# Sums of the scores' stationary quarters moved to DRAM, in a four-layer graph network on one core

## The chip, the cores and the metric

The kernel runs on one core of a Trainium2 chip. The metric is the device time of one execution in microseconds (us). The kernel before has a median of 2388.08 us in three runs (2387.78 to 2389.01). A core has five engines: TensorE (PE; its weight loads are shown apart, as PEld), VectorE (DVE), ScalarE (ACT), GpSimd (POOL) and SyncE (SP), and 16 DMA engines. SP does nothing here but issue DMAs.

## The reference

The input is a matrix `x` of 2708 nodes with 512 features and a symmetric 0/1 matrix `adj` with few ones. Four layers follow each other, and each is `x = layernorm(x + layer(x))`:

```
deg = max((adj != 0).sum(-1), 1)
layer 0: relu((dinv * (adj + I) * dinv @ x + x) @ W + b)       # the degree enters by dinv = rsqrt(deg)
layer 1: (dis[:, None] * adj * dis[None, :] @ x) @ W.T + b
layer 2: twice:  Wh, Ws = split(x @ W)
                 a = softmax(Wh @ Ws.T) * adj
                 x = leaky_relu(a @ Wh + x)
layer 3: adj @ (x @ W) + b, eight heads side by side
```

The change touches layer 2, the two attention layers, and a few instructions after layer 3.

## The kernel before, in words

**Tiles and chunks.** The 2708 nodes are 22 blocks of 128 rows (the last has 20). Columns are cut into six chunks (`CH`): four of 512, one of 384, one of 276. Nearly all SBUF is one pool, `pages`: 87 buffers of 2 KB in each of the 128 partitions. Every large tile takes a page by `self.page(...)` and gives it back after its last access. A second pool of 11 wider buffers (`wides`) holds what is gathered. PSUM is used as two sets of four banks.

**Order.** The class `Ordered` wraps all engines: each engine keeps its instructions in just the order in which the Python code issues them. As one helper issues everything, nearly all lines of the profile are L71; instructions are told apart by the names of their tiles. Numbers of buffers are left out of the names, so the tile `s1_0_3` of a sum and the score tile `s0_1_3` are both `s`.

**An attention layer.** `project_steps` makes, for each chunk, `wst` (four pages a chunk: the stationary side of the scores, `z @ mixed`) and the rows `z`, which go to DRAM (`pairs`). For the scores, the product of `wst` with a moving chunk `xs` is done, for chunks 0 to 4, with seven half products instead of eight (`product`, `PRODUCTS`). For that, `wst` is seen as quarters a11, a12, a21, a22, and `sum_weights` makes three sums, s1 = a21 + a22, s2 = s1 - a11, s4 = a12 - s2. A fourth, s3 = a11 - a21, overwrites a21 (`replace`), whose old content is kept in DRAM (`quarter`) and fetched back by `restore` before chunk 5, which is done with plain products (`scores`). Each of the four wide groups of blocks (k = 0 to 3) has one page each for s1, s2 and s4, so 12 pages hold sums from the projection to the end of chunk 4. Groups 4 and 5 have theirs in one page each.

**The loop of the scores.** `layer` runs over the six chunks, and `pair_steps` over the pairs of blocks, two pairs to a wide group, ten pairs a chunk. A pair is seven products on TensorE (tiles `spx`, `spy`), with ScalarE's copies to the score pages `s` and `v` between. Product 1 comes first, then the older pair's 7, then 2 and 5 (5 reads s1), then the older pair's 4, then 6 (s2) and 3 (s4). Beside it, the chunk before is softened: VectorE subtracts the maximum, ScalarE takes the exponential, VectorE sums it and multiplies by the mask `a`, and SP writes the result to `pairs` in DRAM (`pairs<-s`). When the whole chunk is written, POOL gathers rows of `pairs` by indirect DMAs (`g<-pairs,givers`, some 42 a chunk), and TensorE multiplies them (`acc<-g`, `weigh`). At most ten gathers are ahead of their products. `load_moving` fetches the next chunk's `xs`, `load_mask` the masks.

**The end.** The flags that `examine` leaves in `bad` tell whether the input is of the form that this program supports. After layer 3 `other_weights` sums them: `tensor_reduce` over a row, a product with a float32 matrix of ones `every` (L467, L471) over the partitions, `flag` (L473). All engines load the flag (L474) and branch over the general program (L2196), and a closing barrier follows (L2234). `every` lies in a pool of its own, which is opened after the others are closed.

Of the kernel before, what the change touches and what calls it, by code (L numbers as in the profile page):

```python
# [8 lines left out]
FP = mybir.dt.float32  # L9
FR = mybir.dt.float32r  # L10
BF = mybir.dt.bfloat16
# [8 lines left out]
P = 128  # L20
# [33 lines left out]
class Ordered:  # L54


    def __init__(self, tc):
        self.tc, self.last = tc, {}
        for name in ("tensor", "vector", "scalar", "gpsimd", "sync"):
            setattr(self, name, OrderedEngine(self, getattr(tc.nc, name)))  # L60
# [27 lines left out]
class Kernel:  # L88
# [369 lines left out]
    def other_weights(self):  # L458


        nc = self.nc
        with (
            self.tc.tile_pool(name="ps_bad", bufs=1, space=PSUM) as ps_bad,
            self.tc.tile_pool(name="all", bufs=1) as pool,
        ):
            every = pool.tile([P, P], FP, tag="every", name="every")
            nc.vector.memset(every, 1.0)  # L467
            total = self.small.tile([P, 1], FP, tag="bad_sum", name="bad_sum")
            nc.vector.tensor_reduce(total, self.bad, AX.X, ALU.add)
            ps = ps_bad.tile([P, 1], FP, tag="bad", name="bad_ps")  # L470
            nc.tensor.matmul(ps, every, total, start=True, stop=True)  # L471
            flag = self.small.tile([P, 1], I32, tag="flag", name="flag")
            nc.vector.tensor_scalar_min(flag, ps, 1.0)  # L473
        return nc.values_load(flag[0:1, 0:1])  # L474
# [8 lines left out]
def pairs_of(k):  # L483


    return {4: (1, P), 5: (1, P)}.get(k, (2, 2 * P))


SOFT = NB + 2
ALONE = 18  # L490
SEVEN = [k for k in range(len(CH)) if CH[k][1] >= 384]
# [909 lines left out]
class AttentionLayer:  # L1401
    def __init__(self, number, pairs):
        self.number, self.pairs = number, pairs
        self.w, self.mixed, self.xt, self.wst = [], [], {}, {}
        self.sums, self.second, self.plain = {}, {}, set()


class Attention:
# [7 lines left out]
    def __init__(self, fast):  # L1416
        self.f, self.k, self.nc = fast, fast.k, fast.nc
        self.page, self.bank = fast.page, fast.bank
        tc = self.k.tc
        self.scratch = self.k.ctx.enter_context(  # L1420
            tc.tile_pool(name="pairs", bufs=1, space=DRAM)
        )

        self.pairs = [
            [
                self.scratch.tile([NP, 2 * PAIR + D], FP, tag=f"p{a}{b}", name=f"pairs{a}{b}")
                for b in range(2)
            ]  # L1430
            for a in range(2)
        ]
        self.mixed = self.scratch.tile([DC, P, D], FP, tag="mixed", name="mixed")
        self.quarter = [
            [
                self.scratch.tile(
                    [2, P, pairs_of(k)[0] * P], FP, tag=f"q{a}_{k}", name=f"quarter{a}_{k}"
                )
                for k in range(len(CH))
            ]  # L1440
            for a in range(2)
        ]
        self.layers = [AttentionLayer(a, self.pairs[a]) for a in range(2)]
        self.clock, self.fetch_free, self.pending = 0.0, 0.0, []
# [143 lines left out]
    def sum_weights(self, ly, k):  # L1588

        nc, a = self.nc, ly.number
        wide = pairs_of(k)[0] * P
        a11, a21, a12, a22 = self.quarters(ly, k)
        names = ("s1", "s2", "s4")
        if k < 4:
            tiles = {n: self.page(f"{n}_{a}_{k}", FP, (P, 2, wide)) for n in names}
            tiles = {n: [t[:, c, :] for c in range(2)] for n, t in tiles.items()}
        else:
            t = self.page(f"s12_{a}_{k}", FP, (P, 4, P))  # L1600
            free = CH[k][1]
            tiles = {
                "s1": [t[:, c, :] for c in range(2)],
                "s2": [t[:, 2 + c, :] for c in range(2)],
                "s4": [ly.wst[k][c][:, free : free + P] for c in range(2)],
            }
        for c in range(2):
            nc.vector.tensor_add(tiles["s1"][c], a21[c], a22[c])
            nc.vector.tensor_sub(tiles["s2"][c], tiles["s1"][c], a11[c])
            nc.vector.tensor_sub(tiles["s4"][c], a12[c], tiles["s2"][c])  # L1610
            nc.sync.dma_start(self.quarter[ly.number][k][c], a21[c])
        ly.sums[k] = {"a11": a11, "a12": a12, "a22": a22, "s3": a21, **tiles}
        ly.plain.add(k)

    def replace(self, ly, k):
        if k in ly.plain:
            ly.plain.remove(k)
            t = ly.sums[k]
            for c in range(2):
                self.nc.vector.tensor_sub(t["s3"][c], t["a11"][c], t["s3"][c])  # L1620
# [51 lines left out]
    def pair_steps(self, ch):  # L1672


        nc, h, cw = self.nc, ch.half, ch.cw
        pairs = [(k, b) for k in range(len(CH)) for b in range(pairs_of(k)[0])]
        blocks = lambda p: [CH[p[0]][0] // P + p[1] + i * pairs_of(p[0])[0] for i in range(2)]
        old = None

        def begin(p):  # L1680
            name = f"{ch.name}_{p[0]}_{p[1]}"
            t = {
                "x": self.bank(0, f"spx{name}")[:, :h],
                "y": None,
                "v": self.page(f"v{name}"),
                "j": blocks(p),
                "p": p,
                "name": name,
            }
            for i, j in zip(("s", "r"), t["j"]):  # L1690
                t[i] = ch.s[j] = self.page(f"s{ch.name}_{j}")
            return t

        def seven(t):
            self.product(ch, t["p"], 7, t["x"])
            nc.scalar.copy(t["v"][:, :h], t["x"])

        def four(t):
            self.product(ch, t["p"], 4, t["x"])
            nc.scalar.copy(t["r"][:, :h], t["x"])  # L1700

        def first_block(t):
            nc.vector.tensor_add(t["s"][:, :cw], t["s"][:, :cw], t["y"][:, :cw])
            ch.complete.append(t["j"][0])

        def second_block(t):
            nc.vector.tensor_add(t["r"][:, h:cw], t["r"][:, h:cw], t["v"][:, :h])
            ch.complete.append(t["j"][1])

        for p in pairs:  # L1710
            self.replace(ch.ly, p[0])
            t = begin(p)
            self.product(ch, p, 1, t["x"], start=True)
            nc.scalar.copy(t["s"][:, :h], t["x"])
            yield "mid"
            if old:
                seven(old)
            t["y"] = self.bank(0, f"spy{t['name']}")
            self.product(ch, p, 2, t["y"][:, :h], start=True)
            self.product(ch, p, 5, t["y"][:, h:cw], start=True)  # L1720
            nc.scalar.copy(t["r"][:, h:cw], t["y"][:, h:cw])
            if old:
                first_block(old)
            yield "end"
            if old:
                four(old)
            yield "mid"
            self.product(ch, p, 6, t["x"])
            nc.scalar.copy(t["s"][:, h:cw], t["x"])
            self.product(ch, p, 3, t["y"][:, h:cw])  # L1730
            if old:
                second_block(old)
            old = t
            yield "end"
        seven(old)
        yield "mid"
        first_block(old)
        four(old)
        second_block(old)
        yield "end"  # L1740
# [190 lines left out]
    def fetch_ahead(self):  # L1931
        count = sum(len(c.fetched) for c in self.chunks)
        for c in self.chunks:
            while c.to_fetch:
                if c.softened < SOFT or count >= self.AHEAD:
                    return
# [129 lines left out]
    def layer(self, ly, chunks, fill):  # L2066
        f = self.f
        self.chunks, self.made = chunks, {}
        for k, ch in enumerate(chunks):
# [4 lines left out]
            for what in self.walk(ch):  # L2074
                if what == "mid":
                    if old and n >= 2 and old.softened < SOFT:
                        self.soften(old)
# [8 lines left out]
                if old and n >= 3:  # L2086
                    for _ in range(n % 3 == 0 if ch.seven else 1 + n % 2):
                        if old.softened < SOFT:
                            self.soften(old)
# [21 lines left out]
                if old and n == 2:  # L2111
                    self.shift_columns(old)
            assert not old or old.softened == SOFT
        last = chunks[-1]
# [13 lines left out]
        done = self.clock + (2 if ly.number == 0 else 4)  # L2128
        while last.softened < SOFT:
            self.soften(last)  # L2130
# [107 lines left out]
```

## Time and profile before

| | |
|---|---|
| median of three runs | 2388.08 us |
| the profiled execution: its own time | 2392.95 us |
| its span, first to last instruction | 2391.1 us |
| mean granted TensorE clock | 0.976 |
| TensorE busy | 2250.5 us, 94% of the span |
| VectorE, ScalarE, POOL busy | 1544.5, 723.8, 709.0 us |
| moved by DMA | 491.80 MB, mean 206 GB/s |

The numbers are of one execution. The profile shows for each engine when it was busy and what ended its idle time before an instruction ("a <- b" in the view of the waits: a waited, b released it). The chain of waits goes back from the last instruction, at each step to what released it. Along the span, layers 0 and 1 take until about 595 us, the projection of the first attention layer until 760, its scores until 1280, the second's projection until 1490, its scores and weighing until about 2070, and layer 3 the rest.

### The profile page before, as it was taken

What the parts mean: (1) busy time and instruction counts of PE and PEld (TensorE: products, weight loads), DVE (VectorE), ACT (ScalarE), POOL (GpSimd) and SP (SyncE); (2) the same over time, 40 slices, a digit from 0 to 9 for tenths busy, and PEclk for the clock granted to TensorE, in tenths of its full rate; (3) what the DMA queues carried; (4) which work ended last, traced back from release to release, by engine and by line L of the source; (5) the groups of instructions that cost most, each with busy time, mean ns of one, the idle gap of its engine ahead of it and who ended that gap; (6) DMA issues with size and microseconds to landing.
All of it is one profiled execution on the core that took longest, in us unless ns stands there. A gap on an engine that the chain in (4) does not pass through costs nothing.

```text
span 2391.1 us, 29254 instructions
## 1 busy us (share of the span) xinstructions
PE 2250.5 (94%) x9725; PEld 1523.5 (64%) x9725; DVE 1544.5 (65%) x3180; ACT 723.8 (30%) x1654; POOL 709.0 (30%) x827
## 2 busy tenths in 40 slices
PE   9999999999999998898989999998989896899996
PEld 6767866778445876566764445876565763376684
DVE  6777787776746598666964512588788975355423
ACT  7443442222111242232322101243233322151211
POOL 2433511111000003544456440002635464543000
PEclk9999999999999999999999999999999998999998
DMA  9976732225476036767789998225968889784310
GB/s 342 278 202 183 219 104 78 77 75 190 161 260 254 10 100 204 266 232 241 267 300 333 340 401 315 71 75 173 296 207 267 273 286 317 238 258 139 108 55 32
DMA packets 267858, 491.80 MB, mean 206 GB/s; under 512 B 41006, under 2 KB 132838, under 8 KB 267696
## 3 DMA queue, kind: packets, MB, share of 16 engines
q1 hardware_dynamic: 199040, 274.87, 33.3%
q0 software_dynamic: 68656, 214.96, 28.1%
q8 instruction: 78, 1.28, 0.2%
q14 instruction: 84, 0.69, 0.1%
HBM read 310.17 MB, written 179.54 MB: 205 GB/s over the span
## 4 chain that ended last, share of the span: by engine, by line
PE 74%; DVE 12%; issue 5%; DMA 4%; another core or an unknown queue 2%; ACT 2%; POOL 1%; SPq 0%; DVEq 0%; POOLq 0%; ACTq 0%
PE acc L71 30%; PE spx L71 11%; PE mm L71 8%; PE spy L71 7%; PE wst L71 6%; PE z L71 6%; DVE s L71 4%; PE sp L71 3%; DVE sum L71 2%; DVE top L71 1%; DMA at<-in_adj_t 1%; DMA x<-in_x 1%; POOL g L71 1%; DMA pairs<-s 1%
## 5 line engine op out<-in xcount | busy, mean ns | idle before, releaser
L71 POOL DMA_INDIRECT g<-pairs,givers x510 | 527.3, 1034 | 962.0 <-PE acc L71 283.7
L71 PE MATMUL acc<-m,xh 128*128 128x512 f32 (+4 forms) x1584 | 566.0, 379 | 2.5 <-ACT m L71 1.6
L71 PE MATMUL acc<-m,xl 128*128 128x512 f32 (+4 forms) x1584 | 549.8, 365 | 6.3 <-DVE xl L71 6.3
L71 PEld LDWEIGHTS acc<-m,xh 128*128 128x128 f32 (+1 forms) x1584 | 288.3, 188 | 64.2 <-issue 19.2
L71 PEld LDWEIGHTS acc<-m,xl 128*128 128x128 f32 (+1 forms) x1584 | 288.6, 188 | 50.7 <-DVE xl L71 6.7
L71 PE MATMUL acc<-g 128*32 128x512 f32 (+1 forms) x1020 | 280.6, 621 | 11.2 <-DMA g<-pairs,givers 9.5
L71 PE MATMUL mm<-w,ht 128*128 128x512 f32 (+1 forms) x528 | 223.1, 593 | 0.0
L71 PE MATMUL spx<-xs,wst_sb 128*128 128x256 f32 (+1 forms) x800 | 192.7, 380 | 19.2 <-ACT s L71 15.7
L71 ACT CAST m<-at 128x512 fp32r<-128x512 uint8 (+5 forms) x396 | 198.8, 566 | 37.0 <-DMA at<-mask 27.3
L71 ACT COPY s<-spx 128x256 f32<-128x256 f32 (+1 forms) x300 | 107.0, 360 | 334.8 <-PE spx L71 219.9
L71 DVE TENSOR_TENSOR s<-s,a 128x512 f32<-128x512 f32 (+3 forms) x264 | 166.0, 629 | 48.5 <-DMA a<-mask 24.5
L71 ACT ACTIVATE s<-s 128x512 f32<-128x512 f32 (+3 forms) x264 | 152.2, 581 | 132.1 <-DVE s L71 119.0
L71 PEld LDWEIGHTS spx<-xs,wst_sb 128*128 128x128 f32 x800 | 148.8, 195 | 67.8 <-issue 23.3
L71 DVE TENSOR_TENSOR sum<-sum,s 128x512 f32<-128x512 f32 (+4 forms) x252 | 156.7, 622 | 49.2 <-ACT s L71 26.8
L71 PEld LDWEIGHTS acc<-g 128*32 128x32 f32 (+1 forms) x1020 | 79.2, 137 | 143.7 <-issue 103.5
L71 PEld LDWEIGHTS mm<-w,ht 128*128 128x128 f32 (+1 forms) x528 | 95.7, 186 | 116.5 <-issue 112.2
L71 DVE TENSOR_TENSOR s<-s,shift 128x512 f32<-128x512 f32 (+3 forms) x264 | 162.3, 619 | 9.2 <-ACT shift L71 4.9
L71 PE MATMUL z<-w,xt 128*128 128x512 f32 (+1 forms) x352 | 152.2, 598 | 0.0
L71 DVE TENSOR_TENSOR top<-top,s 128x512 f32<-128x512 f32 (+4 forms) x240 | 149.5, 623 | 2.3
L71 PE MATMUL wst<-xt,mixed 128*128 128x512 f32 (+2 forms) x384 | 150.9, 545 | 0.0
L71 PE MATMUL spx<-t,wst_sb 128*128 128x256 f32 (+1 forms) x400 | 107.8, 394 | 43.4 <-ACT v L71 27.2
L71 PE MATMUL sp<-xs,wst_sb 128*128 128x276 f32 (+5 forms) x512 | 131.3, 460 | 12.2 <-ACT s L71 12.1
(190 smaller groups left out, 2713.3 us busy)
## 6 DMA issues: line engine op xcount, KB each, us to landing
pairs<-z_sb SPq DMA_DIRECT2D x84, 768.0 KB
pairs<-s SPq DMA_DIRECT2D x168, 256.0 KB
at<-in_adj_t SPq DMA_DIRECT2D x84, 256.0 KB
xres<-x POOLq DMA_DIRECT2D x44, 256.0 KB
x<-o POOLq DMA_DIRECT2D x43, 256.0 KB
pairs<-s SPq DMA_DIRECT2D x84, 128.0 KB
a<-mask SPq DMA_DIRECT2D x40, 256.0 KB
x<-x SPq DMA_DIRECT2D x37, 256.0 KB
```

The lines of the kernel that those rows point to most:

```text
L71: ins = call(*args, **kw)
```

## The change

Two things are edited.

First, s1, s2 and s4 of groups 0 to 3 are written to DRAM while chunk 0 of the layer runs (`keep_sums`, 12 writes of 256 KB a layer), in `pair_steps` at the first pair of each group. In chunks 1 to 4 they are no longer held in SBUF: `load_sums` takes three new pages for a group and fetches them. Group k + 1 is fetched in the first pair of group k, behind product 5, and group 0 of the next chunk in the last pair of a chunk. These are 12 loads of 256 KB a chunk, 48 a layer, all issued by SP. The number of pages stays 87.

Second, `other_weights` uses the bfloat16 matrix of ones that exists from the start (`ones_b`) instead of `every`; the sums of flags are cut to at most 1 and written as bfloat16 before the product.

```diff
@@ other_weights
         with (
             self.tc.tile_pool(name="ps_bad", bufs=1, space=PSUM) as ps_bad,
-            self.tc.tile_pool(name="all", bufs=1) as pool,
         ):
-            every = pool.tile([P, P], FP, tag="every", name="every")
-            nc.vector.memset(every, 1.0)
-            total = self.small.tile([P, 1], FP, tag="bad_sum", name="bad_sum")
+            sums = self.small.tile([P, 2], FP, tag="bad_sum", name="bad_sum")
+            total, some = sums[:, 0:1], sums[:, 1:2].bitcast(BF)[:, 0:1]
             nc.vector.tensor_reduce(total, self.bad, AX.X, ALU.add)
+            nc.vector.tensor_scalar_min(some, total, 1.0)
             ps = ps_bad.tile([P, 1], FP, tag="bad", name="bad_ps")
-            nc.tensor.matmul(ps, every, total, start=True, stop=True)
+            nc.tensor.matmul(ps, self.ones_b, some, start=True, stop=True)
@@
+STREAMED = 4
@@ AttentionLayer.__init__
-        self.sums, self.second, self.plain = {}, {}, set()
+        self.sums, self.streamed, self.plain = {}, {}, set()
@@ Attention.__init__
+        self.sums = [
+            [
+                self.scratch.tile([3, P, 2, 2 * P], FP, tag=f"u{a}_{k}", name=f"sums{a}_{k}")
+                for k in range(STREAMED)
+            ]
+            for a in range(2)
+        ]
@@ sum_weights
-        if k < 4:
-            tiles = {n: self.page(f"{n}_{a}_{k}", FP, (P, 2, wide)) for n in names}
-            tiles = {n: [t[:, c, :] for c in range(2)] for n, t in tiles.items()}
+        if k < STREAMED:
+            ly.streamed[k] = [self.page(f"{n}_{a}_{k}", FP, (P, 2, wide)) for n in names]
+            tiles = {
+                n: [t[:, c, :] for c in range(2)] for n, t in zip(names, ly.streamed[k])
+            }
@@
+    def keep_sums(self, ly, k):
+
+        for n, t in enumerate(ly.streamed[k]):
+            self.nc.sync.dma_start(self.sums[ly.number][k][n], t)
+
+    def load_sums(self, ly, k):
+
+        for n, name in enumerate(("s1", "s2", "s4")):
+            t = self.page(f"{name}_{ly.number}_{k}", FP, (P, 2, 2 * P))
+            self.nc.sync.dma_start(t, self.sums[ly.number][k][n])
+            ly.sums[k][name] = [t[:, c, :] for c in range(2)]
+
@@ pair_steps
+        groups = [p[0] for p in pairs if p[0] < STREAMED and p[1] == 0]
+        following = ch.k + 1 in SEVEN
         for p in pairs:
             self.replace(ch.ly, p[0])
+            if ch.k == 0 and p[0] < STREAMED and p[1] == 0:
+                self.keep_sums(ch.ly, p[0])
             t = begin(p)
...
             nc.scalar.copy(t["r"][:, h:cw], t["y"][:, h:cw])
             if old:
                 first_block(old)
+            if ch.k and p[1] == 0 and p[0] + 1 in groups:
+                self.load_sums(ch.ly, p[0] + 1)
+            if following and p == pairs[-1]:
+                self.load_sums(ch.ly, 0)
             yield "end"
```

## The prediction

> **What bounds the kernel now.** I read the parts of the page in order: engines, slices, queues, chain.
>
> ```profile
> PE 2250.5 (94%) x9725; PEld 1523.5 (64%) x9725; DVE 1544.5 (65%) x3180; ACT 723.8 (30%) x1654; POOL 709.0 (30%) x827
> ...
> DMA  9976732225476036767789998225968889784310
> ...
> q1 hardware_dynamic: 199040, 274.87, 33.3%
> q0 software_dynamic: 68656, 214.96, 28.1%
> ...
> PE 74%; DVE 12%; issue 5%; DMA 4%; another core or an unknown queue 2%; ACT 2%; POOL 1%; SPq 0%; DVEq 0%; POOLq 0%; ACTq 0%
> ```
>
> TensorE carries the span: 94% busy, 74% of the chain. The DMA engines are at 6 to 9 tenths in the attention layers. The change touches two stretches of those layers, and I asked for their busy times (columns: stretch, length, busy time of each engine, granted clock, DMA share, GB/s).
>
> ```profile
> 880.00:1210.00 330.00, 292.20 (x1323) 211.72 (x1322) 248.06 (x430) 102.39 (x255) 141.91 (x137) 0.94 0.72 238
> 1620.00:1940.00 320.00, 288.79 (x1293) 202.54 (x1291) 265.03 (x473) 100.09 (x245) 154.01 (x145) 0.97 0.77 256
> ```
>
> TensorE is idle for 38 and 31 us there. The view of the waits says for whom (columns: total, times, longest); first TensorE, whole span, then ScalarE and POOL in 880 to 1210.
>
> ```profile
> PE acc L71 <- DMA g<-pairs,givers: 9.5, 13, 2.2
> PE bad_ps L471 <- DVE every L467: 7.2, 1, 7.2
> ```
>
> ```profile
> POOL g L71 <- PE acc L71: 80.7, 15, 24.0
> POOL g L71 <- PE spx L71: 40.9, 9, 20.8
> ACT s L71 <- remote: 35.5, 7, 9.7
> ```
>
> TensorE hardly waits for gathers; gathers wait for TensorE to free their buffers. "Remote" is a wait whose end no instruction explains. It is the candidate for a wait for pages, so I tested it. Each tile's address is known from the built program, and the trace has its accesses. For each re-use of a page I took the start of the first write less the end of the former tile's last access. In 890 to 1210 and 1620 to 1940 there are 386 re-uses: the median is 12 to 16 us, the shortest 1.9. Where a copy behind a long remote wait opens a page, that page had been free for 12 to 22 us. **Pages are not what anything waits for there.**
>
> The tail is last, from the chain and from the lines of its branch and closing barrier:
>
> ```profile
> 2376.24 1.97 DMA out<-o
> ...
> 2378.65 0.18 DVE every L467
> ...
> 2379.02 0.57 PE bad_ps L471 x2
> ...
> 2379.62 0.16 DVE flag L473
> ```
>
> ```profile
> L2196 PEldq COMPARE_BRANCH  x1: 3358/3358/3358, 2380.4 to 2380.4; - x1
> ```
>
> The memset of `every` waits for the last output to land, because its pool takes memory of the closed ones. The flag is at 2379.8, all engines branch at 2380.4, and none goes on before 2384.1.
>
> **What the Trainium skill says.** "DMA: Bandwidth & Descriptors", section "Issuing engines are not separate DMA queues": whoever starts a DMA, all run on the same 16 engines and interleave. The trace agrees: while gathers (POOL) hold 0.5 to 0.66 of the engines, SP's transfers get only the rest. "Runtime: NRT & Kernel Launch", section "Instruction fetch mechanics": a taken branch out of the fetched window stops its engine until the target is fetched. The trace agrees: 3.7 us between branch and next instruction on each engine. "TensorE: Matmul & The Clock Gate", section "Part 1: The HAM clock gate": about 3.4 us of idleness halve TensorE's clock for a window. The trace shows 0.5 for 3.4 or 6.8 us near such gaps (985 and 1101 us).
>
> **The change, part by part.**
>
> *Flags.* The order of the changed program puts the sum of flags at its old early place (it runs at 759.5), one tiny minimum after it, the matmul right behind the last `mm` (ends 2371.9), and the flag on VectorE behind the first residual add of the last chunk (ends 2373.3). So the flag is there at 2373.5 and the last row is 0.2 later. POOL, free since long, loads and branches 6.3 us earlier, at 2374.1. From its branch to the end of its last drain it took 9.86 us (2380.39 to 2390.24, of it 4.3 the drain), and 0.85 to the span's end: 2384.8. The others: `o` 2376.4, load 0.5, branch 2377.1, refetch 3.7, SP's waits and drain 1.5: 2382.4, earlier than POOL. **-6.3 us.** If the drain runs from SP's arrival instead (3.6 us later, as now), -4.3; if only the wait for the memset goes, -3.1; -7.5 is the most.
>
> *Writes and loads.* Per layer 12 writes in chunk 0 and 12 loads in each of 4 chunks, all 256 KB: 120 SP issues at some 0.37 us (SP's `a<-mask` took 0.37 to 0.5 each), 44 us of a queue that waits 475 us for VectorE's `s`. DMA time of one: q1 moved 274.87 MB in 33.3% of 2391.1 us, 345 GB/s, so 0.76 us of all 16 engines; 2.3 us for the three of a group. Queued behind them on SP are the writes of `s`, the masks and `xs`; POOL's first gather waits for the last such write.
>
> I put each group of loads where SP stands just before it, and compared with the product that needs it. The lead is 7.6 to 31 us, and some 60 for the first two groups of chunk 1. SP's transfers land 4.5 us after issue (median; one in ten over 8.5). In chunks 1 to 4 the groups 0 and 2 fall into stretches without gathers, where 2.3 us of free DMA time come within 3 to 4 us: hidden. Lateness of all 32 groups: **+1** (0 to 6).
>
> *Gathers.* Groups 1 and 3 in chunks 2, 3 and 4 of both layers fall among gathers and find their 2.3 us only after 11 to 47 us. So gathers land up to 2.3 us later. For groups 1 those are the first ten of a chunk, which lie ready 23 us and more before TensorE takes them: nothing. For groups 3 the shortest margins are 2.5, 1.6, 3.9, 1.2, 1.0 and 4.1 us; lateness past them sums to 3.1. **+3** (0 to 14, if all six are passed on).
>
> *The remote waits.* They hold 11.1% and 3.7% of the chain in the two stretches, 48 us, all while gathers run. What they are I can't tell. Loads add 18.9 MB to the 160 MB moved there, 12%; if they grow so, +6; if they are chance, below nothing. **+2** (-5 to +10).
>
> *TensorE's queue.* 35 more semaphore waits; one took 51 ns: **+1** (0 to 1.8). New gaps at half clock: **+1** (0 to 4).
>
> *Pages.* Nine pages are freed, the shortest margins grow from 2 to over 4 us and nobody waited: **0** (-5 to 0). Outside chunks 1 to 4 order and pages are the same.
>
> Sum: -6.3 + 1 + 3 + 2 + 1 + 1 = +1.7. Against the profiled execution (span 2391.1, its own time 2393.0): 2394.7. That execution was 4.9 us above the median of the runs, so on their scale 2388.1 + 1.7 = **2389.8**.
>
> **The rivals.**
>
> *Slower: gathers become the bound.* One mechanism: in the second half of chunks 2 to 4 the DMA engines are full, and each load pushes the gathers back. Price: 12 groups x 2.3 = 27.6 us if all is passed on; half of it and the remote waits' +6 give 2388.1 - 6.3 + 14 + 6 + 3 = 2405. For it: nearly full DMA engines at 944 to 965 and 1055 to 1079, margins of 1 to 4 us. Against: margins of 23 us in groups 1. It decides from margins under 2.3 us in most windows.
>
> *Faster: all loads hidden.* The transfers vanish in free slots, and only the tail is left: 2388.1 - 6.3 = 2382. For it: leads of 7.6 us and more. Against: the full windows of groups 3.
>
> *The pages did bind.* If the remote waits were pages, up to 40 us go: 2342. Against: margins of 12 us and more at just those copies.
>
> *It doesn't do what it says:* loads late because SP is stuck behind a write of `s`. Ten groups with leads under 10 us, 3 us each: 2388.1 - 6.3 + 30 = 2412.
>
> **How the numbers follow.** A measurement of this kernel can tell 0.2%, 4.8 us, from no change: 2383.3 to 2392.9. The forecast, the tail's gain eaten by the loads: 0.43, own range 2383 to 2393. Slower by full gathers 0.28, by late loads 0.05. Faster by hidden loads 0.22, by pages 0.02. The range leaves out the pages and the worst of the slower cases: 2381 to 2404.
>
> **What would show it.** Right: in the chain `every` is gone and the flag stands at some 6 us before its old place relative to the last `o`; waits of TensorE for `s<-sums` stay under 6 us in total; waits for `g` grow by some 3; remote waits stay near 54 us. Wrong: the remote waits shrink by tens of microseconds, then pages did bind; TensorE waits for `s` loads by over 10 us; the end of the span doesn't move relative to the last `o`.

## The result, and the profile after

The kernel after has a median of 2384.86 us in 20 runs, the kernel before 2384.90 us in 20 runs beside it: **ratio 1.0000, 95% interval 0.9979 to 1.0021, no difference**. A second comparison, in the experiments, gave 0.9989 (0.9974 to 1.0004); weighted by their intervals the two make 0.9993 ± 0.0012, that is -1.7 ± 2.9 us. A single run scatters far more than the three runs at the start let one think: 2375 to 2400 us before, 2365 to 2397 after. A part of this comes from ahead of the change: in the fourteen profiles of this case the first product of the scores begins at 762.5 to 773.5 us, and the edits hardly touch what runs before. So the experiments stand on medians with intervals, and on waits of single executions only where these stand out of that scatter.

The profiled execution of the kernel after took 2388.23 us (span 2386.2). First its page: engines, slices, queues, chain.

```profile
PE 2251.1 (94%) x9724; PEld 1522.3 (64%) x9724; DVE 1544.5 (65%) x3180; ACT 726.2 (30%) x1654; POOL 711.2 (30%) x827
...
DMA  9976832225478137877899999426978889785211
...
q1 hardware_dynamic: 216320, 306.34, 37.3%
q0 software_dynamic: 68656, 214.96, 28.1%
...
PE 75%; DVE 12%; issue 5%; DMA 3%; another core or an unknown queue 2%; ACT 1%; POOL 1%; SPq 0%; DVEq 0%; ACTq 0%; POOLq 0%
```

TensorE does the same work in the same share of the span. What is new is in q1: 31.5 MB more, 120 transfers of 256 KB, and one or two tenths more in the DMA slices of the attention layers. The two stretches (stretch, length, busy time of each engine, granted clock, DMA share, GB/s):

```profile
880.00:1210.00 330.00, 291.04 (x1303) 208.40 (x1301) 247.32 (x426) 100.83 (x251) 139.53 (x135) 0.95 0.79 265
1620.00:1940.00 320.00, 287.01 (x1294) 203.16 (x1293) 267.51 (x477) 101.84 (x249) 151.99 (x143) 0.97 0.84 282
```

The DMA share rises by 0.07 in both. TensorE is busy for 1.2 and 1.8 us less in them, too little to tell from scatter in one execution. The waits (total, times, longest): TensorE over the whole span, then POOL and ScalarE in 880 to 1210.

```profile
PE acc L71 <- DMA g<-pairs,givers: 10.8, 13, 2.3
```

```profile
POOL g L71 <- PE acc L71: 81.6, 16, 23.7
```

```profile
ACT s L71 <- remote: 27.5, 6, 9.1
```

Gathers still wait for TensorE, hardly TensorE for gathers. (Its weight loads, PEld, do wait for `g`, 36.7 us before and 43.6 after, but beside a matmul that is still busy: ahead of the products with `g` TensorE stands idle for 11.2 and 12.8 us in all.) No wait of TensorE for `s<-sums` exists: every load is there in time. The remote waits of ScalarE's `s` are 54.9 us over the span, 54.5 before: what was freed is not what these copies waited for. What they do wait for is in the last section.

The end does move. The chain's last lines, and the lines of the branch (line, queue, operation, count, min/median/max ns, first and last start):

```profile
2375.42 0.14 DVE flag L472
...
2377.87 0.55 DVE o L71
```

```profile
L2225 POOLq COMPARE_BRANCH  x1: 53/53/53, 2376.4 to 2376.4; - x1
...
L2225 SPq COMPARE_BRANCH  x1: 50/50/50, 2379.4 to 2379.4; - x1
L2225 POOLq INC_SWDGE_SEM  x1: 1235/1235/1235, 2379.7 to 2379.7; - x1
```

`every` is gone, the flag is there before the last `o` (relative to it, 6.4 us earlier than before), and POOL branches 3 us ahead of SP. From the end of the last `o` (2378.4) to the end of the span it is 7.7 us; before it was 14.9. Yet the whole execution is only 4.9 us shorter than the profiled one of before: the last `o` itself comes 2.2 us later. This is the question for the experiments: is the zero a gain and a loss of one size?

### The profile page after: what moved, and what is told of

The parts are those of the page before. It is cut to its first block, busy times and chain, and to the rows that moved or that the text cites. A ratio compares the mean times of both kernels' runs of the same rounds, so it can differ in the third digit from the quotient of the medians.

```text
span 2386.2 us, 29469 instructions
## 1 busy us (share of the span) xinstructions
PE 2251.1 (94%) x9724; PEld 1522.3 (64%) x9724; DVE 1544.5 (65%) x3180; ACT 726.2 (30%) x1654; POOL 711.2 (30%) x827
## 4 chain that ended last, share of the span: by engine, by line
PE 75%; DVE 12%; issue 5%; DMA 3%; another core or an unknown queue 2%; ACT 1%; POOL 1%; SPq 0%; DVEq 0%; ACTq 0%; POOLq 0%
PE acc L71 31%; PE spx L71 11%; PE mm L71 8%; PE spy L71 8%; PE z L71 6%; PE wst L71 6%; DVE s L71 4%; PE sp L71 2%; DVE sum L71 2%; DVE top L71 1%; DMA g<-pairs,givers 1%; PE mix L71 1%; DMA a<-mask 1%; POOL g L71 1%
## 5 line engine op out<-in xcount | busy, mean ns | idle before, releaser
L71 PEld LDWEIGHTS acc<-m,xh 128*128 128x128 f32 (+1 forms) x1584 | 288.2, 188 | 64.7 <-issue 18.6
L71 PE MATMUL acc<-g 128*32 128x512 f32 (+1 forms) x1020 | 286.8, 614 | 12.8 <-DMA g<-pairs,givers 10.8
L71 PE MATMUL sp<-xs,wst_sb 128*128 128x276 f32 (+5 forms) x512 | 130.1, 457 | 11.5 <-ACT s L71 11.4
```

Of the source, the lines that this page charges most:

```text
L71: ins = call(*args, **kw)
```

## The experiments

My theory: the flags gain 6 to 7 us at the end, the streaming takes them back in chunks 1 to 4, and the freed pages are worth nothing. Rivals: the gathers become the bound; the pages did bind, and the loads hide that gain; loads and flags are both free. Three groups of kernels ran, each beside runs of the kernel before, whose medians were 2387.6, 2385.4 and 2315.0 us. Ratios are taken within a group; where two are subtracted, their intervals are added as squares.

### Each edit alone

The flags alone are the kernel before with the second edit of the diff; the streaming alone is the kernel after with the same edit taken back. Its main line (the rest is left out here):

```diff
-            nc.tensor.matmul(ps, self.ones_b, some, start=True, stop=True)
+            nc.tensor.matmul(ps, every, total, start=True, stop=True)
```

> The kernel before with the second edit alone (bfloat16 ones and the minimum in other_weights). Theory (the tail gains, the loads take it back): from the end of the last write of `o` to the end of the span it takes 7.7 us as in the kernel after, instead of 14.9, so 6 to 7 us less than before, ratio 0.997. Rival (the tail gains nothing on the whole, because POOL's drain runs from SP's arrival): the flag is early, but the end stands 10 us and more after the last `o`, ratio 0.999 to 1. Rival (the loads are free and the tail's gain is only that of one profiled execution): the same time as the kernel after, ratio 1.

> The kernel before with the first edit alone (sums to DRAM and back); the flags keep the float32 `every`. Theory: 7 us above the kernel before if the medians of 20 runs are right (2384.86 is 0 off, and the tail gave -7), 2 to 8 us with the spread of single executions, ratio 1.001 to 1.003; the end 14.9 us after the last `o`. Rival (gathers become the bound): 14 to 28 us above, ratio 1.006 to 1.012, with TensorE's waits for `g` of 20 us and more. Rival (loads are hidden): ratio 1. Rival (pages did bind): below 1 by the shrinking of ScalarE's remote waits from 54 us.

Flags alone: 2378.59 us, **ratio 0.9965 (0.9946 to 0.9985)**. Streaming alone: 2397.67 us, **ratio 1.0029 (1.0007 to 1.0050)**. Together -0.0006, and the kernel after, at -0.0007, shows just that. In the profile of the flags alone the last `o` ends at 2377.4 and the span at 2384.9, 7.5 us; with the streaming alone the chain ends as before:

```profile
2388.85 0.18 DVE every L467
...
2389.22 0.57 PE bad_ps L471 x2
...
2389.82 0.16 DVE flag L473
```

The flag starts 11.5 us before the span's end (2401.3), with all branches still to come. So the zero is a sum: -8.4 us ± 4.8 and +6.9 us ± 5. That loads are hidden, and that gathers cost 14 to 28 us, both fall; so does a net gain by pages.

The traces put both parts where they belong, free of the scatter ahead of the scores. From the first product of the scores to the last product with gathered rows it takes 1414.0 us (before) and 1406.2 (flags alone), and 1416.6 (after) and 1413.5 (streaming alone): about 5 us more with the streaming, if single executions tell so little. From there to the end it takes 214.2 us in all three profiles with the old flags, and 206.8 to 207.6 in all eleven with the new ones.

### More traffic: each load twice

```diff
             self.nc.sync.dma_start(t, self.sums[ly.number][k][n])
+            for d in range(1):
+                spare = self.page(f"x{d}{name}_{ly.number}_{k}", FP, (P, 2, 2 * P))
+                self.nc.sync.dma_start(spare, self.sums[ly.number][k][n])
```

> The kernel after, with each of the 96 loads of sums issued twice, the second into a page of its own that nobody reads. It doubles the suspected cost of the transfers: 25 MB more, 0.76 us of all DMA engines for each load, 73 us in all, and 96 more issues on SP. Theory (part of the loads falls on gathers with little margin): the cost of the loads is a few microseconds and as much again or up to twice it comes on top, +5 to +14 us against the kernel after; TensorE's waits for `g` rise from 10.8 to 15 to 25 us. Rival (loads hidden in free DMA time): +0 to +2, waits for `g` unchanged. Rival (gathers are the bound): +28 us. Rival (the cost is SP's queue, loads late): TensorE waits for `s<-sums` appear, 10 us and more.

Ratio 1.0013 (0.9993 to 1.0033), +0.0020 ± 0.0023 against the kernel after: +5 us ± 6. TensorE's waits for `g` stay as they were:

```profile
PE acc L71 <- DMA g<-pairs,givers: 11.3, 13, 2.3
```

The gathers as the bound are out, and so is the lateness of loads, for which no wait of a matmul shows. The mechanism that I had put first for the streaming's cost, gathers of groups 3 pushed past their margins, does not show either. What grows are TensorE's waits for VectorE's `s`, from 2.0 to 8.1 us, in short pieces.

### The freed pages taken away again

In `restore`, twelve pages (all groups, shown here) or six (groups 1 and 2) are kept until chunk 4:

```diff
+        for t in ly.streamed.pop(k, []):
+            self.nc.vector.tensor_copy(t[:1, 0, :1], t[:1, 0, :1])
```

> The kernel after, but the 12 pages that hold the sums in chunk 0 are kept until chunk 4, by a one-element copy of each onto itself on VectorE when its group is restored (24 tiny copies, some 0.1 us each). So the loads stay and the freed pages are taken away; with the pages of the loads 3 to 6 fewer are free than in the kernel before. Theory (pages don't bind): same as the kernel after within 3 us; TensorE's and ScalarE's waits as there. Rival (freed pages gain something that the loads' cost hides): slower than after by that gain, 7 us and more, and SP's loads or ScalarE's copies wait longer for pages, remote waits of ScalarE above 60 us.

> The kernel after with six of the freed pages kept until chunk 4 (those of groups 1 and 2; one-element copies onto themselves as in the run that held twelve). With the 3 to 6 pages of the loads the scores have 9 to 12 pages taken by sums, never more than the 12 of the kernel before. It is the undoing of what the change frees, without the shortage of the run that held twelve. Theory (the freed pages were spare): the kernel after within its spread, ratio to before 0.998 to 1.002; no copy of ScalarE waits for a write of `s` to land in 880 to 1210. Rival (the freed pages gain what the loads cost elsewhere): +5 us and more, ratio 1.002 to 1.006.

Twelve held: 2416.63 us in six runs, **ratio 1.0118 (1.0077 to 1.0160)**. ScalarE's waits in 880 to 1210 name the shortage:

```profile
ACT s L71 <- DMA pairs<-s: 5.3, 3, 4.0
ACT v L71 <- DMA pairs<-s: 2.8, 1, 2.8
```

A copy opens a page whose former content is just being written to DRAM, and starts when that write has landed. In both attention layers these waits sum to 23.2 us in 11 places, against 1.4 us in one place in the kernel before, in the kernel after, and with six held (4.2 us with the streaming alone). SP waits for such writes as well, 34.4 us in the two stretches (18.6 of it ahead of loads of sums), against 0.8 in the kernel after. The remote waits don't grow (44.5 us for `s`): a shortage of pages looks different from them. So this is no proof that pages did bind: with twelve held and 3 to 6 for the loads the scores have fewer pages than before. It shows how near the edge is, within six pages. (By the same count the change frees 6 to 9 pages at a time, not always nine.)

Six held: 2376.92 us, ratio 0.9966 (0.9947 to 0.9986). Taking the spare pages away loses nothing, so having them gains nothing. But that is 0.0027 ± 0.0023 below the kernel after, and I expected 0. So I repeated the contrast on the other base, beside the kernel after itself:

> The kernel before with the streaming alone (flags as before), and the six freed pages of groups 1 and 2 held until chunk 4. It repeats the contrast of the run with six held pages on the other base. Streaming alone was 1.0029. Theory (pages are spare, the low run was chance): 1.002 to 1.004. Rival (freed pages start something earlier that collides, so that holding them takes the cost away): 0.999 to 1.001.

> The kernel after itself, unchanged, beside the other three on one chip. The run that held six freed pages gave 0.9966, the first comparison of the kernel after 1.0000, the flags alone 0.9965. Theory (streaming costs 7 us, and the run with six pages was low by chance): 0.999 to 1.001 again. Rival (holding six pages really takes the cost of streaming away): the same here, 0.999 to 1.001, but then the run of streaming alone with six pages held stands at 1.000. Rival (streaming costs less than the two first comparisons say): 0.997 to 0.999.

Streaming alone with six held: **1.0027 (1.0013 to 1.0042)**, the same as the 1.0029 without. Kernel after: 0.9989 (0.9974 to 1.0004), at the border between the theory and the last rival. Holding six pages takes no cost away; the low 0.9966 I put down to chance, without having shown it. If held pages make no difference, the streaming's cost is now known twice: weighted 1.0028 ± 0.0012, **+6.5 us ± 3**.

### Where the loads cost: half of the groups

```diff
-STREAMED = 4
+STREAMED = (1, 3)
```

The tests for a number below `STREAMED` become tests for being in it; the second kernel has (0, 2).

> The kernel after, but only groups 1 and 3 are streamed; groups 0 and 2 keep their six pages. These are the loads that fall among gathers in chunks 2 to 4. My prediction put the cost of streaming there (+3 and what the remote waits grow), so theory A: nearly all of the 7 to 8 us, ratio to before 0.999 to 1.000. Theory B (cost by number of loads, wherever they stand): half, ratio 0.998. Rival (hidden): that of the flags alone, 0.9965.

> The kernel after, but only groups 0 and 2 are streamed, whose loads mostly fall into stretches without gathers. Theory A (hidden there): as with the flags alone, ratio 0.9965 to 0.9975. Theory B (cost by number of loads): 0.998. Rival (page shortage is what costs, since here and in the run with groups 1 and 3 six pages stay taken): both of these runs above the kernel after, 1.002 and more.

Groups 1 and 3: ratio 0.9981 (0.9961 to 1.0000). Groups 0 and 2: 0.9968 (0.9944 to 0.9992). Against the flags alone that is +0.0016 ± 0.0028 and +0.0003 ± 0.0031. The order is that of theory A, but neither is told from the other or from half each: inconclusive. That the streaming costs by a shortage of pages is out: then both would have been above 1.002.

### Bytes or issues

Three DMAs more behind each load, from DRAM to DRAM, touch no page. Once they move 256 KB each, once 8 KB; of the second edit only the inner line is shown:

```diff
             self.nc.sync.dma_start(t, self.sums[ly.number][k][n])
+            for d in range(3):
+                self.nc.sync.dma_start(self.spare[n][d], self.sums[ly.number][k][n])
```

```diff
+                self.nc.sync.dma_start(
+                    self.spare[n][d][:16, 0, :P], self.sums[ly.number][k][n][:16, 0, :P]
+                )
```

> The kernel after, with three more DMAs behind each load of sums, on SP too, which copy the same 256 KB from DRAM to a spare place in DRAM that nobody reads. No page is touched: 288 more issues on SP and 75 MB more read (and written) in the same places as the loads, three times the traffic of the change's loads without what TensorE waits for. Theory A (the 7 to 8 us of the streaming are DMA traffic that pushes gathers and score writes): three times as much again, +20 to +25 us against the kernel after, ratio 1.008 to 1.010 to before, TensorE's waits for `g` above 20 us. Theory B (they come from what hangs on the loads: more waits in TensorE's queue, the order of pages, stalls that become half-clock windows; double loads gave only +3): +0 to +9 us, ratio 1.000 to 1.004. Rival (SP's queue becomes the bound, since each load brings four issues): score writes and first gathers of a chunk are late, +25 us and more.

> As in the run with three DRAM copies behind each load, but each copy moves 16 rows of 512 bytes (8 KB) instead of 256 KB. SP's issues stay (288 more), the traffic goes (2.4 MB). There the time was 2423 us, 37 us above the kernel after; SP's waits for VectorE's `s` in 880 to 1210 and 1620 to 1940, the spare time of its queue, had shrunk from 277 to 131 us, VectorE waited 32 us for masks, and the waits for `g` were unchanged. Theory A (the bytes did it: masks and loads land later): within 5 us of the kernel after, ratio to before 0.998 to 1.003, no waits of VectorE for masks. Theory B (SP's queue did it, each load bringing four issues): most of the 37 us stays, ratio 1.008 and more, SP's waits for `s` as small as there, and VectorE's waits for masks.

256 KB each: 2422.93 us in six runs, **ratio 1.0149 (1.0115 to 1.0182)**, 37 us ± 9 above the kernel after. 8 KB each: **1.0035 (1.0017 to 1.0053)**, against 0.9989 for the kernel after in the same group, so +0.0046 ± 0.0023 or 11 us ± 5. Neither theory has it whole: the issues alone cost 11 of 37, the bytes the rest, some 26 us. (The two runs are of different groups, so the split is rough.)

Whom do they hit? TensorE's waits with 256 KB copies, while DMA engines are 93% busy in both stretches:

```profile
PE spx L71 <- DVE s L71: 26.9, 10, 9.2
...
PE acc L71 <- DMA g<-pairs,givers: 10.8, 12, 2.4
...
PE spy L71 <- DMA s<-sums: 6.9, 2, 4.7
```

Not the gathers. TensorE waits for VectorE's `s` and for late loads; with the smaller groups of both that is 36.9 us, against 2.0 in the kernel after, and the time grew by 37. The longest of these waits shows the way there (start, length, engine, operation, and in brackets how long the engine had waited for what):

```profile
1180.08 2.21 SPq L71 DMA_DIRECT2D spare<-sums  x3
...
1184.94 0.32 SPq L71 DMA_DIRECT2D a<-mask  x1
...
1197.37 0.69 DVE L71 TENSOR_TENSOR s<-s,a 128x512 f32<-128x512 f32 x1 [14.17 <-DMA a<-mask]
...
1198.59 2.93 PE L71 MATMUL spx<-xs,wst_sb 128*128 128x192 f32 x8 [9.18 <-DVE s L71]
```

SP issues a mask behind three copies, it lands 12.3 us later, VectorE has waited for it, and TensorE for VectorE. A second wait of this kind, of 8.3 us, stands at 1945. Over the whole span VectorE waits 57.0 us for masks, against 25.0 in the kernel after. With 8 KB copies the same waits grow, but the way from one to the next does not show: VectorE waits 59.7 us for masks, against 44.3 in the kernel after of that group, and TensorE 8.0 us for VectorE's `s` and for loads, against 1.7, in short pieces away from the masks. These are single executions.

SP's queue has its spare time in its waits for VectorE's `s`, here in 880 to 1210: first the kernel before, the kernel after, and that with 256 KB copies:

```profile
SPq L71 <- DVE s L71: 171.9, 55, 18.4
```

```profile
SPq L71 <- DVE s L71: 129.8, 49, 18.5
```

```profile
SPq L71 <- DVE s L71: 60.7, 37, 3.4
```

In the third group, the kernel after and that with 8 KB copies:

```profile
SPq L71 <- DVE s L71: 162.1, 78, 13.9
```

```profile
SPq L71 <- DVE s L71: 91.6, 56, 4.2
```

The view counts only waits whose end the trace names, and the third group's traces name more of them, so the groups can't be set against each other here. SP was never full: its issues, added up from the trace, take 60, 80 and 138 us of these 330, and 158 with 8 KB copies.

From the end of the issue to the last landing on record, worked out from the trace in both stretches: one in ten writes of `s` takes over 5.4 us before, 6.7 after, 7.8 with double loads, 10.2 with 256 KB copies; a gather's median goes from 4.0 to 4.3, 4.7 and 5.7 us. In the third group it is 8.6 us for the writes after and 10.4 with 8 KB copies, at nearly the same DMA shares. Gathers become slower too, but TensorE's waits for them don't grow: ten are ahead.

### The lead of the loads

```diff
-            if ch.k and p[1] == 0 and p[0] + 1 in groups:
+            if ch.k and p[1] == 1 and p[0] + 1 in groups:
```

> The kernel after, with group k + 1 fetched in the second pair of group k instead of the first, so that each of these loads stands one pair of blocks later on SP; group 0 is left where it is. The loads land 4.3 us after their issue (median; one in ten 8.9) and the shortest lead in the first place was 7.6 us. Theory (lateness costs nothing now because the lead is as long as it is): TensorE waits for `s<-sums` appear, 10 to 40 us in total over 24 groups, and the time is 5 to 30 us above the kernel after. Rival (the lead has slack of a whole pair): same time as the kernel after, no such waits; then fewer pages are in use at a time at no cost.

Ratio 1.0014 (1.0000 to 1.0028), against 0.9989 for the kernel after: +0.0025 ± 0.0021, 6 us ± 5. TensorE's waits:

```profile
PE acc L71 <- DMA g<-pairs,givers: 11.7, 24, 1.3
...
PE spy L71 <- DMA s<-sums: 8.3, 6, 2.2
```

Lateness appears, 8.6 us with one wait of `spx`, just under what I expected, and the median moves by about as much. But the profiled execution that shows these waits took 2310.94 us, no longer than the kernel after's 2311.63. And another wait, of ScalarE for pages, came with them:

```profile
ACT s L71 <- DMA pairs<-s: 8.1, 4, 4.1
```

It was 1.4 us in the kernel after. So the full lead is enough, and a shorter one makes loads late; that the lateness is what the 6 us are, is not shown.

## Why the prediction was right, point by point

2389.8 us was forecast, 2384.9 measured, and "no difference" was the likeliest case. Of the 4.9 us between, 3.2 is the base: three runs had a median of 2388.1, twenty had 2384.9. The rest is the sum, +1.7 forecast and 0.0 measured (both comparisons together -1.7 ± 2.9).

- *Flags, -6.3.* Right, and a little small. From last `o` to end it is 14.8 to 14.9 us in the three profiles with the old flags and 7.5 to 8.3 in the eleven with the new ones. So some -7.1, in the timed runs -8.4 ± 4.8. POOL was last as forecast: its drain of 4.3 us follows its own arrival. What I had too long is POOL's refetch: 2.9 us from branch to next instruction (2376.42 to 2379.31), where the forecast had taken over the 3.9 of before (2380.39 to 2384.25).
- *Late loads, +1.* Right: no wait of TensorE for them in two profiles of the kernel after.
- *Gathers, +3.* Wrong as a mechanism. TensorE's waits for `g` are 7.8 to 12.0 us in all profiles, with DMA shares from 0.72 to 0.93 in the first stretch. I took the lateness past single margins as if each were passed on. That gathers land later is right; the step that failed is from there to TensorE.
- *SP's queue, at nothing beyond lateness.* This is the term that was mis-sized. I had 44 us of issues against 475 us of waiting and gave them no price. The 288 tiny copies cost 11 us, 37 ns each; at that price the change's 120 issues are an estimated 4.4 us. With the large copies the way goes over masks and VectorE to TensorE. That issues cost the change as much as they cost there, and by this way, is my reading and not shown: in the kernel after TensorE waits 2.0 us for VectorE's `s`, before 1.7, with the streaming alone 4.0.
- *Remote waits, +2.* They did not respond: 54.5 us for `s` before, 54.9 after, 37.9 with the flags alone, 38.5 with the streaming alone. They are scatter between executions, and no price of loads; the last section shows what they are.
- *TensorE's semaphore waits +1, half clock +1.* The first was not measured by itself. For the second the mean granted clock of the timed runs is lower by 0.0007 ± 0.0012 with the streaming alone, and by 0.0009 ± 0.0007 with six pages held as well, each against the kernel before in its group. If what is missing is at half clock, 0.0009 is an estimated 4.4 us more of it and a loss of up to 2.2 us: not in conflict, and hardly told from nothing.
- *Pages, 0.* Right, from margins of 2 us and more. The run with twelve held shows that the margin was thin.

So the two halves were right in sign and size, and so was the balance between them. But the streaming's +8 met the measured +6.5 ± 3 partly by luck: of the 8, the 3 for gathers and the 2 for remote waits did not show, and what SP's queue costs stood at nothing. Where the change's own 6 us arise, wait by wait, stays open: in one execution they are lost among remote waits of some 50.

The best version is the flags alone, 0.9965. With groups 0 and 2 streamed too it is 0.9968, not told apart from it; that gives up six pages, of which the loads take three or more back at a time.

## What to carry to other kernels

Where a change has two parts, price and run each alone: a zero can be -8 and +7, and then one half is worth keeping. Before counting on freed memory, look for somebody who waits for it, and take it away again to see how far off the shortage is. The large copies here hit what stood behind them in their own queue, the masks, and not the largest consumer with the longest lead: follow the queue's next transfers to whoever waits for them. And compare a stretch from one piece of work to another, as from the first product of the scores to the last with gathers; it leaves out scatter that arises elsewhere.

## What the hardware showed that I had not expected

In the third group the same kernels took 3% less: the kernel before 2315.0 instead of 2387.6 us, the kernel after 2311.7 instead of 2384.9. The chain of the kernel after shows what is missing:

```profile
PE 71%; DVE 12%; DMA 11%; issue 3%; ACT 2%; POOL 0%; SPq 0%; DVEq 0%; ACTq 0%; POOLq 0%
```

"Another core or an unknown queue" is gone, and in its view of the waits there is not one remote wait. Its busy times in the same stretches:

```profile
880.00:1210.00 330.00, 320.76 (x1503) 230.74 (x1502) 275.87 (x487) 115.84 (x285) 166.04 (x156) 0.99 0.88 305
1620.00:1940.00 320.00, 295.22 (x1336) 200.85 (x1336) 275.60 (x515) 110.26 (x263) 175.07 (x163) 0.98 0.90 309
```

TensorE is busy for 321 of 330 us instead of 291, at a clock of 0.99 instead of 0.95, and the DMA engines move 305 instead of 265 GB/s. (The same stretch holds more of the work there.) The instructions are the same and in the same order. The loss lies in the attention layers alone: from the first product of the scores to the last with gathers it takes 1416.6 us in the first profile of the kernel after and 1337.2 in that of the third group.

What the remote waits are can be read from the traces. Semaphores are the counters by which engines release each other. In the ten profiles that have such waits, every one of the 293 ends with a count on the same semaphore, which only TensorE's instructions raise; the last product that raises it had ended 1.5 to 7.4 us earlier by the profile. So these are neither waits for another core nor for pages, but for TensorE. One of them in the kernel after:

```profile
1094.27 1.03 PE L71 MATMUL spx<-xs,wst_sb 128*128 128x256 f32 x4
...
1100.11 0.37 ACT L71 COPY s<-spx 128x256 f32<-128x256 f32 x1 [9.11 <-remote]
...
1101.33 2.08 PE L71 MATMUL spx<-xs,wst_sb 128*128 128x256 f32 x4 [6.03 <-ACT s L71]
```

The product should end at 1095.3, its copy starts 4.8 us later, and TensorE then has to wait for ScalarE. At 1100.5 a period of half clock begins. In the third group no count of TensorE in the attention layers comes later than 0.13 us, TensorE is idle for 66.1 us of the span instead of 122.9, and its clock is halved for 41 us instead of 100.

Why the counts come late (or the products end later than the profile has it) stays open. The traces with late counts are also those that lack records: some 30% of the landings of DMAs and 11 to 14% of TensorE's counts, where the third group's lack under 1%. Whether the recording holds the engines up, no run here tests. The groups ran some 25 minutes apart, and the record gives the same chip number for all three. The waits are not the edits': they come and go with the group. I had spent a term of the sum and a rival on them.
